# A chain of matrix products in sets: one round instead of two between the steps, and fewer sets under way

## The chip, the core and the metric

The kernel runs on one core of a Trainium2 chip, in one launch. The metric is the time of the launch in device microseconds; the median of three runs is compared. The core has five engines that run side by side, each in the order of its own instructions: TensorE (PE in the profile, with its weight loads as PEld), VectorE (DVE), ScalarE (ACT), GpSimd (POOL) and SyncE (SP), which only issues transfers here. An engine's instruction that needs another engine's result waits for it, and all that stands behind it on the same engine waits too.

## The reference

The input `x` has 32 images of 32 channels, each a 128 x 128 matrix, in float32. Two layers:

```python
def _L0_conv_ref(A):                      # NUM_ITER = 5
    normA = jnp.sqrt(jnp.sum(A2 * A2, axis=(1, 2)))
    Y = A2 / normA[:, None, None]
    Z = jnp.broadcast_to(I, A2.shape)
    for _ in range(NUM_ITER):
        T = 0.5 * (3.0 * I - jnp.matmul(Z, Y))
        Y = jnp.matmul(Y, T)
        Z = jnp.matmul(T, Z)
    return Y * jnp.sqrt(normA)[:, None, None]
...
x = x + _L0_conv_ref(_gn(x))
x = x + _L1_conv_ref(_gn(x), L1_conv_weights1, L1_conv_weights2)
```

`_gn` normalises each group of two channels by its mean and variance. The first layer is a Newton iteration towards the square root of each of the 1024 matrices. The second takes the real part of a two-dimensional Fourier transform, multiplies 32 x 32 low modes at two corners by weights that mix the channels, and transforms back.

## The kernel before

**Sets.** Four channels of an image are one set: 256 sets, eight to an image. `newton` (line 398) does the first layer for one set. It is a Python generator: each `yield` ends a step, and the loop that makes the program resumes many generators in turn, so that the yields decide in which order the instructions of different sets stand in the queues of the engines. Nothing of this runs on the chip: it is the order that is fixed here.

**Lanes and rounds.** The main loop (line 1000) counts rounds. In a round it visits the `LANES` = 9 lanes in turn. A free lane takes the next set if it is due: `due` grows by `FAR` = 27/9 or `NEAR` = 25/5 rounds with each start, and among near sets fewer than `LESS` = 5 may be under way. An occupied lane's generator is resumed once. A step that ends with `yield from rest` pauses for two rounds, since `rest = (None, None)`. At lane 1 of each round `step(preps)` is called, at lane 2 `step(specs)`, at lane 3 `step(posts)`, at lane 0 `step(prods)` in two rounds of three and `step(backs)` in the third.

**Far and near.** Sets of images 1 to 18 are far: 144 of them, the first stage. Image 0 (8 sets) and images 19 to 31 (104 sets, the second stage) are near. They differ in one transposition of the iteration, `quartic` (line 362), which is run twice in a set: a far set does it by a transposition of blocks on VectorE and a trip through DRAM, out and back on SP's queue; a near set on TensorE.

**The steps of a set**, with the names that the trace gives to the product (all products are line 305 but one; each is 8 matmul instructions in the trace, L415 with 256 columns, transpositions 4):

- mb by m (`ps<-x,b`), evicted to v by VectorE (L280); the second time `ps<-my,mb`
- far: v turned by VectorE (L371, `turn<-v`), stored to DRAM (L373), a pause, loaded back into w (L384, or four issues of L381), a pause, then on GpSimd w + r (L386). Near: v transposed on TensorE (L311, `ps<-ident,v`), evicted with r added to w by VectorE (L280)
- v by w (`ps<-w,v`), evicted to q by VectorE (L280)
- q by m (`ps<-x,q`), evicted to y by ScalarE (L404)
- q by y (`ps<-my,q`), evicted to m by ScalarE (L407)
- m transposed (L311, `ps<-ident,my`), evicted to mb by ScalarE (L272); GpSimd adds the scaled identity to it, r (L292 or L299)
- the second quartic, then q by y and m at once (L415, `ps<-my,q`), evicted by ScalarE in two instructions (L418) and four (L421)
- w by q (`ps<-q,t`), evicted to t by VectorE (L280)
- t by y (`ps<-y,t`), added to the input xt by VectorE (L425).

There is a pause after each of them, in the far quartic one more after each leg of the trip. A far set has 27 yields, a near one 25.

**Around the sets.** `fetch` loads a set's inputs on ScalarE's queue, `staged` scales them on ScalarE and GpSimd ahead of its start. `prep` (line 185) makes the statistics of two images at once: 16 steps with a load of xs on ScalarE's queue, three steps ahead, and two `bn_stats` (L206), then small steps with two square roots (`root`, line 151). `stage` (line 940) starts a `prep` when a set 12 before its images is staged, and finishes it at once, step by step, if it isn't done when its image is staged. `settle` stores a finished set to DRAM (L433), folds it on GpSimd (L438) and takes its statistics on VectorE (L443); `forward`, `summed` and `spectrum` (posts and specs) transform it. When a group of images is done (`GROUPS` = 20, 7, 3, 2), its spectra are multiplied by the weights (prods: `wide_products`, `small_products`, `last_products`) and transformed back (backs: `inverse`), between the near sets that still run. `weights` (line 751) loads the last group's weights on SP's queue into buffers as the last sets give them up: its `kinds` name a buffer and the round of the last set from which it is free.

Buffers come from pools with counts by name (`rooms`, line 256); until set 158 an extra pool is added to them.

Of the kernel before, what the change touches and what calls it, by code (L numbers as in the profile page):

```python
# [37 lines left out]
B = 32  # L38
C = 32
G = 16  # L40
LANES, LESS = 9, 5
FAR, NEAR = 27 / 9, 25 / 5
GROUPS = (20, 7, 3, 2)


# [6 lines left out]
FIRST = GROUPS[0] - 1  # L52
# [16 lines left out]
def conv_preact_kernel(  # L69
# [56 lines left out]
    early = first.enter_context(tc.tile_pool(name="early", bufs=1, side="right"))  # L126
# [16 lines left out]
    tail = False  # L143
# [7 lines left out]
    def root(v, n, tag):  # L151

        s0 = small.tile([P, n], F32, tag="root_0", name=f"{tag}_s0")
        nc.scalar.activation(s0, v, AF.Sqrt)
        q = small.tile([P, n], F32, tag="root_1", name=f"{tag}_q")
        nc.vector.reciprocal(q, s0)
        nc.vector.tensor_mul(q, q, v)
        nc.vector.tensor_tensor(q, q, s0, ALU.add)
        s = small.tile([P, n], F32, tag=f"{tag}_s", name=f"{tag}_s", bufs=2)
        nc.vector.tensor_scalar_mul(s, q, 0.5)  # L160
        return s
# [23 lines left out]
    def prep(bs, made):  # L185

        n = len(bs)
        nc_, ng = n * C, n * G
# [27 lines left out]
        v = small.tile([P, nc_ + ng], F32, tag="a_v", name=f"a_v{first_b}")  # L216
# [4 lines left out]
            vg, v[:, 0:nc_].rearrange("p (g c) -> p g c", c=2), AX.X, ALU.add  # L221
        )
        nc.vector.tensor_scalar(v[:, nc_:], vg, 0.5, EPS, ALU.mult, ALU.add)
        s = root(v, nc_ + ng, "a_r")
        iv = small.tile([P, nc_ + ng], F32, tag="a_inv", name=f"a_inv{first_b}")
        nc.vector.reciprocal(iv, s)
        yield
# [3 lines left out]
        nn = small.tile([P, ng, 2], F32, tag="a_d", name=f"a_n{first_b}")  # L231
# [5 lines left out]
        )  # L237
        nn = nn.rearrange("p g c -> p (g c)")
        nc.vector.tensor_scalar_mul(nn, nn, P * (1.5 / (EYE * QF)) ** 2)
        sn = root(nn, nc_, "a_t")  # L240

        off = small.tile([P, ng, 2], F32, tag="a_off", name=f"a_off{first_b}", bufs=2)
        nc.vector.tensor_tensor(
# [118 lines left out]
    def quartic(m, mb, r, far, more, wide):  # L362


        v = plus(m, -QA * MS, products(mb, m), "v", more)
        if far:


            t = four("turn", more)
            form = "p c (b i) -> p b c i" if wide else "p c (i b) -> p b c i"  # L370
            nc.vector.transpose(blocks(t), v.rearrange(form, b=4))  # L371
            held = dram.tile([P, 512], F32, name="turn", tag="turn", bufs=8)
            kept(nc.sync.dma_start(out=held, in_=t.rearrange("p c x -> p (c x)")))  # L373
            yield from rest
            w = four("w", more)
            wb = blocks(w).rearrange("p a c j -> p a (c j)")
            if wide:
                for b in range(4):
                    rows = slice(32 * b, 32 * b + 32)
                    src = held[:, P * b : P * b + P].rearrange("(a i) x -> i a x", a=4)  # L380
                    kept(nc.sync.dma_start(out=wb[rows], in_=src))  # L381
            else:
                src = held.rearrange("(a i) (b x) -> (i b) a x", a=4, b=4)
                kept(nc.sync.dma_start(out=wb, in_=src))  # L384
            yield from rest
            nc.gpsimd.tensor_tensor(w, w, r, ALU.add)  # L386
            w = blocks(w).rearrange("p a c j -> p c a j")
        else:
            yield from rest
            w = plus(transposed(v), 1.0, r, "w", more)  # L390
        yield from rest
        q = plus(products(v, w), QF / (16 * MS**4), eye, "q", more)
        yield from rest
        return q

    rest = (None, None)

    def newton(g, sn, xt, m, mb, r, far, more):

# [84 lines left out]
    def summed(b, st):  # L484
# [15 lines left out]
        v = small.tile([P, 2], F32, tag="b_v", name=f"b_v{b}")  # L500
# [2 lines left out]
        yield  # L503
        s = small.tile([P, 3], F32, tag="b_r", name=f"b_r{b}")
        nc.scalar.activation(s[:, 0:1], v[:, 0:1], AF.Sqrt)
        nc.vector.reciprocal(s[:, 1:2], s[:, 0:1])
        nc.vector.tensor_scalar(
            s[:, 2:3], v[:, 0:1], s[:, 1:2], s[:, 1:2], ALU.mult, ALU.mult
# [2 lines left out]
        r = small.tile([P, 1], F32, tag="b_inv", name=f"b_inv{b}")  # L511
# [4 lines left out]
    def spectrum(b, u):  # L516
# [16 lines left out]
        for i in range(2):  # L533
# [7 lines left out]
        v, r = scales.pop(b)  # L541
# [6 lines left out]
            AF.Identity,  # L548
            scale=r,
        )  # L550
        nc.vector.scalar_tensor_tensor(
            spec[0:C, 0, 0, 0:1], v[0:C, 1:2], r[0:C], spec[0:C, 0, 0, 0:1], ALU.mult, ALU.add
        )
        yield
        i, j = where[b]
# [195 lines left out]
    def weights():  # L751


        kinds = [("b", 2)] * 3 + [("x", 2), ("b", 4), ("x", 4), ("x", 10)]
        kinds += [("my", 11)] * 2 + [("r", 12)] * 4 + [("mb", 15)] * 2 + [("v", 15)] * 2
        kinds += [("w", 16)] * 2 + [("my", 16), ("r", 17)] + [("q", 19)] * 3
        first = B * C // 4 - 10
        spare = []
        for half in range(4, 2 * KK):
# [64 lines left out]
    holding = []  # L824
# [94 lines left out]
    posts = []  # L919
    specs = []  # L920
# [10 lines left out]
    rounds = 0  # L931
# [61 lines left out]
            yield  # L993

    preps.append(prep([0], made))
    coming = [((0, 0), [1])] + [((b - 2, 4), [b, b + 1]) for b in range(2, B, 2)]
    fetch(*fetches.pop(0))
    stage()
    fetch(*fetches.pop(0))
    while todo or any(lanes) or posts or specs or prods or backs:  # L1000
        tail = not todo and not any(lanes)
        if early and len(settled) >= MORE:
            change()
        for i in range(LANES):
# [16 lines left out]
            if lanes[i] is not None:  # L1021
# [3 lines left out]
                if next(steps, lanes) is lanes:  # L1025
                    lanes[i] = None
                    end(b, g, xt)
            if i == 1:
                step(preps)
            if i == 2 or tail:  # L1030
                step(specs)
            if i == 3 or tail:
                step(posts)
            if i == 0 and rounds % 3 or tail:
                step(prods)
            if i == 0 and (rounds % 3 == 0 or holding) or tail and not (posts or specs):
                step(backs)
        rounds += 1

# [68 lines left out]
```

## Time and profile before

| | us |
|---|---|
| median of 3 runs | 3051.56 (3039.8 to 3056.13) |
| the profiled run | 3040.36 |
| its span, first to last instruction | 3038.6 |
| mean granted TensorE clock | 0.984 |
| chain that ended last: PE / DMA / DVE | 75% / 10% / 9% of the span |
| DMA | 636.40 MB, mean 209 GB/s |
| POOL before r, waiting for mb (L299 behind ACT L272) | 278.8 in 66 waits |
| SP's queue before L373, waiting for the turned v, 152 to 1545 us | 466.1 in 185 waits |

The chain that ended last is followed back from the last instruction, at each step to what released it. A wait of an engine that isn't the bottleneck costs nothing by itself: SP and GpSimd may stand long before a transfer or an addition as long as the result is there when TensorE wants it. Matmul instructions are pipelined, so PE's busy time counts overlapping instructions once; the starts of two matmuls of the same kind that follow each other lie closer together than one of them lasts. In the timeline one product of eight matmuls is one line, "x8", with its start and the time to its end.

### The profile page before, as it was taken

To read this page: it belongs to the slowest core of one execution; us is meant where nothing else is said; L and a number is where in the kernel's file an instruction comes from. 1 tells how busy PE (TensorE), PEld (TensorE's weight loads), DVE (VectorE), ACT (ScalarE), POOL (GpSimd) and SP (SyncE) were. 2 spreads that over 40 slices of the span, in tenths; PEclk is the share of its full clock that TensorE was granted. 3 is DMA by queue.
4 is the path that set the end of the run, shared out by engine and by line. 5 is a ranking of instruction groups with operands and counts; after the bars stand their busy time and mean duration, and the time that the engine had idled before them with its cause. 6 is when DMAs were issued, how large, how long until landed. Compare 5 with 4: busy or idle time off the path is not lost.

```text
span 3038.6 us, 73447 instructions
## 1 busy us (share of the span) xinstructions
PE 2893.8 (95%) x27076; PEld 2684.5 (88%) x27076; DVE 2219.3 (73%) x4255; ACT 1636.0 (54%) x4187; POOL 1997.6 (66%) x2312
## 2 busy tenths in 40 slices
PE   6999999999999999999999999899999998999994
PEld 6899999999999999999999889798898887899983
DVE  6778787978787878778776745876877765876664
ACT  3565656565655656566544445455454454555552
POOL 4567677667777676777766435667677774677453
PEclk9999999999999999999999999999999999999996
DMA  5476766667675767576742566667667767775676
GB/s 179 148 224 199 220 213 205 212 207 224 197 237 188 251 184 246 185 229 198 228 136 81 183 204 214 232 206 239 229 225 242 245 231 242 227 222 189 198 240 217
DMA packets 476659, 636.40 MB, mean 209 GB/s; under 512 B 97040, under 2 KB 257296, under 8 KB 476304
## 3 DMA queue, kind: packets, MB, share of 16 engines
q1 hardware_dynamic: 363408, 425.88, 43.3%
q10 hardware_dynamic: 112896, 205.83, 21.4%
q8 instruction: 217, 3.56, 0.5%
q14 instruction: 138, 1.13, 0.1%
HBM read 402.42 MB, written 229.11 MB: 208 GB/s over the span
## 4 chain that ended last, share of the span: by engine, by line
PE 75%; DMA 10%; DVE 9%; POOL 2%; issue 2%; ACT 2%; SPq 1%; ACTq 0%; DVEq 0%; POOLq 0%
PE ps L305 49%; PE ps L415 12%; PE ps L311 6%; DMA w<-turn 3%; DMA xs<-in_xs 3%; PE ps L461 2%; PE ps L883 2%; DMA or<-od 1%; PE ps L612 1%; DVE yt L900 1%; PE ps L865 1%; DVE a_st L206 1%; DVE v L280 1%; DVE turn L371 1%; PE ps L682 1%
## 5 line engine op out<-in xcount | busy, mean ns | idle before, releaser
L386 POOL TENSOR_TENSOR w<-w,r 128x512 f32<-128x512 f32 x288 | 366.2, 1275 | 316.2 <-DMA w<-turn 262.1
L305 PE MATMUL ps<-w,v 128*128 128x128 f32 x4096 | 554.4, 279 | 19.0 <-POOL w L386 12.1
L339 ACT ACTIVATE b<-b,a_off,a_sc 128x128 f32<-128x128 f32 x1024 | 467.3, 491 | 177.5 <-issue 45.6
L305 PEld LDWEIGHTS ps<-w,v 128*128 128x128 f32 x4096 | 504.6, 193 | 35.1 <-POOL w L386 16.2
L415 PE MATMUL ps<-my,q 128*128 128x256 f32 x2048 | 493.3, 384 | 7.8 <-DVE q L280 5.2
L280 DVE SCALAR_TENSOR_TENSOR q<-ps,eye 128x512 f32<-128x512 f32 x512 | 348.8, 681 | 187.4 <-PE ps L305 181.1
L438 POOL TENSOR_TENSOR fold<-xt 128x256 f32<-128x256 f32 x512 | 364.3, 732 | 162.8 <-DVE xt L425 133.2
L833 POOL TENSOR_TENSOR yt<-yt,d 128x512 f32<-128x512 f32 x248 | 309.9, 1277 | 174.3 <-ACT d L895 137.7
L415 PEld LDWEIGHTS ps<-my,q 128*128 128x128 f32 x2048 | 373.2, 192 | 53.3 <-DVE q L280 4.7
L346 POOL TENSOR_SCALAR x<-xt,a_nm,a_sc 128x128 f32<-128x128 f32 x736 | 322.3, 450 | 18.3 <-DVE a_n L232 18.3
L299 POOL TENSOR_TENSOR r<-mb,eye 128x512 f32<-128x512 f32 x112 | 142.6, 1274 | 288.6 <-ACT mb L272 278.8
L418 ACT ACTIVATE t<-ps 128x256 f32<-128x256 f32 x512 | 192.6, 384 | 237.3 <-PE ps L415 229.4
L421 ACT ACTIVATE y<-ps,a_t_s 128x128 f32<-128x128 f32 x1024 | 312.4, 372 | 0.0
L305 PE MATMUL ps<-my,q 128*128 128x128 f32 x2048 | 276.7, 278 | 6.0 <-ACT d L895 3.9
L305 PE MATMUL ps<-x,b 128*128 128x128 f32 x2048 | 275.6, 278 | 6.7 <-POOL x L346 5.7
L305 PE MATMUL ps<-my,mb 128*128 128x128 f32 x2048 | 275.9, 278 | 6.5 <-ACT d L895 5.2
L305 PE MATMUL ps<-x,q 128*128 128x128 f32 x2048 | 276.0, 278 | 1.8 <-DVE q L280 1.6
L206 DVE BATCH_NORM_STATS2 a_st<-xs 128x6 f32<-128x256 f32 x512 | 195.4, 412 | 112.6 <-DMA xs<-in_xs 112.0
L305 PE MATMUL ps<-q,t 128*128 128x128 f32 x2048 | 274.5, 277 | 3.2 <-ACT d L895 1.6
L305 PEld LDWEIGHTS ps<-my,q 128*128 128x128 f32 x2048 | 260.8, 193 | 17.4 <-ACT d L895 4.5
L404 ACT ACTIVATE my<-ps 128x512 f32<-128x512 f32 x256 | 152.7, 596 | 229.2 <-PE ps L305 211.1
L305 PE MATMUL ps<-y,t 128*128 128x128 f32 x2048 | 273.9, 277 | 1.9 <-DVE t L280 1.6
(138 smaller groups left out, 5540.3 us busy)
## 6 DMA issues: line engine op xcount, KB each, us to landing
turn<-turn SPq DMA_DIRECT2D x288, 256.0 KB
b<-in_x ACTq DMA_DIRECT2D x256, 256.0 KB
xt<-in_xt ACTq DMA_DIRECT2D x256, 256.0 KB
xs<-in_xs ACTq DMA_DIRECT2D x256, 256.0 KB
mid<-xt SPq DMA_DIRECT2D x256, 256.0 KB
yt<-mid SPq DMA_DIRECT2D x128, 512.0 KB
out<-yt SPq DMA_DIRECT2D x120, 512.0 KB
w<-turn SPq DMA_DIRECT2D x144, 256.0 KB
```

What stands on the lines that cost most here:

```text
L206: nc.vector.bn_stats(st[:, 2 * k + j, :], tiles[k][:, j, :])
L280: nc.vector.scalar_tensor_tensor(s, ps, f, t, ALU.mult, ALU.add)
L305: nc.tensor.matmul(ps[:, j, :], lhsT[:, j], rhs[:, j], start=True, stop=True)
L311: nc.tensor.transpose(ps[:, j, :], t[:, j, :], ident)
L339: nc.scalar.activation(t, x, AF.Identity, bias=offset[:, c], scale=scale[:, c])
L346: nc.gpsimd.tensor_scalar(m[:, j, :], xt[:, j, :], nm[:, c // 2 : c // 2 + 1], sc[:, c : c + 1], ALU.add, ALU.mult,)
L386: nc.gpsimd.tensor_tensor(w, w, r, ALU.add)
L415: nc.tensor.matmul(both[j // 2][:, j % 2], q[:, j], my[:, j], start=True, stop=True)
L418: nc.scalar.mul(w[:, 2 * h : 2 * h + 2, :], both[h][:, :, 1, :], 1 / (MS * QF))
L421: nc.scalar.mul(y[:, j, :], both[j // 2][:, j % 2, 0, :], sn[:, c : c + 1])
L438: nc.gpsimd.tensor_tensor(f[:, :, 64 * half : 64 * half + 64], xt[:, :, 0:64], xt[:, :, 64:128], op)
L833: engine.tensor_tensor(yh, yh, d, op)
```

## The change

All of it is in the order of the instructions; none is added or removed on any engine, and no buffer count changes.

- The pause between steps is one round. The two pauses of the far quartic's trip through DRAM stay at two rounds, under a new name, `trip`.
- Six lanes instead of nine. A far set starts every 3 rounds, as before; a near set every 4 rounds instead of 5, while fewer than four are under way.
- `prep` is stepped in every second round once the first stage's extra pool is gone, and then starts two sets earlier. It has four more steps: before and after each square root on ScalarE. `summed` and `spectrum` have one more step each, after an instruction of ScalarE that VectorE continues.
- The products of the spectra are stepped in four rounds of five, the way back in two of five.
- The rounds from which `weights` may use a buffer follow the shorter life of a set.

```diff
-LANES, LESS = 9, 5
-FAR, NEAR = 27 / 9, 25 / 5
+LANES, LESS = 6, 4
+FAR, NEAR = 3, 4
...
         nc.scalar.activation(s0, v, AF.Sqrt)
+        yield
         q = small.tile([P, n], F32, tag="root_1", name=f"{tag}_q")
...
         nc.vector.tensor_scalar(v[:, nc_:], vg, 0.5, EPS, ALU.mult, ALU.add)
-        s = root(v, nc_ + ng, "a_r")
+        yield
+        s = yield from root(v, nc_ + ng, "a_r")
...
-        sn = root(nn, nc_, "a_t")
+        yield
+        sn = yield from root(nn, nc_, "a_t")
...
             kept(nc.sync.dma_start(out=held, in_=t.rearrange("p c x -> p (c x)")))
-            yield from rest
+            yield from trip
             w = four("w", more)
...
                 kept(nc.sync.dma_start(out=wb, in_=src))
-            yield from rest
+            yield from trip
             nc.gpsimd.tensor_tensor(w, w, r, ALU.add)
...
-    rest = (None, None)
+    rest = (None,)
+    trip = (None, None)
...
         nc.scalar.activation(s[:, 0:1], v[:, 0:1], AF.Sqrt)
+        yield
         nc.vector.reciprocal(s[:, 1:2], s[:, 0:1])
...
             scale=r,
         )
+        yield
         nc.vector.scalar_tensor_tensor(
...
-        kinds = [("b", 2)] * 3 + [("x", 2), ("b", 4), ("x", 4), ("x", 10)]
-        kinds += [("my", 11)] * 2 + [("r", 12)] * 4 + [("mb", 15)] * 2 + [("v", 15)] * 2
-        kinds += [("w", 16)] * 2 + [("my", 16), ("r", 17)] + [("q", 19)] * 3
+        kinds = [("b", 2)] * 3 + [("x", 2), ("b", 3), ("x", 3), ("x", 6)]
+        kinds += [("my", 6)] * 2 + [("r", 7)] * 4 + [("mb", 9)] * 2 + [("v", 9)] * 2
+        kinds += [("w", 9)] * 2 + [("my", 9), ("r", 10)] + [("q", 11)] * 3
...
-    coming = [((0, 0), [1])] + [((b - 2, 4), [b, b + 1]) for b in range(2, B, 2)]
+    coming = [((0, 0), [1])] + [((b - 2, 4 if b < FIRST else 2), [b, b + 1]) for b in range(2, B, 2)]
...
-            if i == 1:
+            if i == 1 and (early or rounds % 2):
                 step(preps)
...
-            if i == 0 and rounds % 3 or tail:
+            if i == 0 and rounds % 5 or tail:
                 step(prods)
-            if i == 0 and (rounds % 3 == 0 or holding) or tail and not (posts or specs):
+            if i == 0 and (rounds % 5 in (0, 2) or holding) or tail and not (posts or specs):
                 step(backs)
```

## The prediction

> **What bounds the kernel now.** I read the busy row first, then the span cut into its stages, then the waits stage by stage, and last the timeline, for what stands between two steps of one set.
>
> ```profile
> PE 2893.8 (95%) x27076; PEld 2684.5 (88%) x27076; DVE 2219.3 (73%) x4255; ACT 1636.0 (54%) x4187; POOL 1997.6 (66%) x2312
> ```
>
> TensorE (PE) is the busiest, but 95% hides two stages:
>
> ```profile
> core 0: us, PE busy (x) PEld busy (x) DVE busy (x) ACT busy (x) POOL busy (x), PEclk, DMA share, GB/s
> 152.00:1545.00 1393.00, 1379.39 (x11507) 1304.72 (x11506) 1109.09 (x2113) 831.38 (x2159) 1004.74 (x1109) 1.00 0.69 214
> 1545.00:1700.00 155.00, 155.00 (x1318) 146.93 (x1317) 105.64 (x223) 75.12 (x194) 86.45 (x117) 1.00 0.32 105
> 1700.00:2900.00 1200.00, 1143.28 (x12345) 1037.81 (x12344) 820.43 (x1543) 607.56 (x1532) 768.51 (x922) 0.99 0.68 222
> 2900.00:3039.00 139.00, 95.95 (x995) 81.95 (x993) 77.56 (x141) 53.55 (x133) 62.54 (x62) 0.81 0.65 226
> 0.00:152.00 152.00, 120.14 (x920) 113.06 (x921) 106.59 (x239) 68.42 (x170) 75.36 (x104) 0.97 0.50 163
> ```
>
> PE idles 14 us in the whole first stage (152 to 1545), 57 in the second (1700 to 2900), 32 at the start, 43 at the end. Nearly all that a faster kernel could gain lies in the second stage, the start and the end; in the first there is nothing to win and a cover to lose.
>
> What the cover is, in the timeline:
>
> ```profile
> 704.69 1.06 PE L305 MATMUL ps<-q,t 128*128 128x128 f32 x8
> ...
> 706.05 0.67 DVE L280 SCALAR_TENSOR_TENSOR t<-ps,eye 128x512 f32<-128x512 f32 x1
> ...
> 710.43 1.05 PE L305 MATMUL ps<-y,t 128*128 128x128 f32 x8
> ```
>
> The product of w and q ends at 705.8, VectorE (DVE) evicts it until 706.7, and the set's next product starts at 710.4: 3.7 us in which the eviction could have come later at no cost. Pairing every eviction with the product that reads it, over the 144 far sets, this slack is 3.4 to 5.4 us in the median at the steps without a trip through DRAM, and 1.5 to 3.3 us at the tenth percentile; at the two products behind a trip it is 3.3 and 3.7 us, and 0.2 and 0.8. Over the 104 later near sets it is 2.7 to 3.7 us, and 0.6 to 2.3. Who sits waiting meanwhile, in the first stage and in the second:
>
> ```profile
> POOL w L386 <- DMA w<-turn: 250.7, 116, 6.2
> ```
>
> ```profile
> DVE a_st L206 <- DMA xs<-in_xs: 39.9, 20, 6.3
> DVE spec L551 <- ACT spec L545: 12.5, 6, 4.5
> ```
>
> **The rounds, counted.** A far set had 27 pauses and one visit in which it ends: 28 rounds, nine lanes, 3.11 rounds a set. Starts lie 10.06 us apart, so a round is 3.23 us. Afterwards 18 pauses and the end make 19 rounds on six lanes, 3.17 a set, 3.18 us a round at the same pace. A step's distance falls from 6.46 to 3.18 us: 3.3 us less. A near set had 25 pauses and the end, five lanes, 5.2 rounds a set; starts lie 13.57 us apart, a round is 2.61 us. Afterwards a set starts every 4 rounds of 3.39 us; the distance falls from 5.22 to 3.39: 1.8 us less. The matrix work itself is unchanged, and so are its evictions, its DMAs and their kinds.
>
> **Far sets (144).** From each measured slack I take 3.3 us and keep what falls below zero. Short are 10 to 20% of most steps, 33% at q (L280, before L415) and 45% at m (ACT L407, before the transposition); of the two trips through DRAM, 50 and 43%. One wait of PE lets all that comes later catch up, so within one round I count the largest shortfall alone: 181 us over the stage without the trips, 357 with them. That is the upper end. The lower is -14, PE's whole idle time there. A count by hand says where in between. If the six lanes are taken in turn, the products follow each other as: mb by m of a new set, w by q, q by y, then t by y of the set whose w by q was just done. One product issues in 0.90 us (in the timeline the next starts at 1022.62 after 1021.72), so 1.80 us after the first ends PE wants t. VectorE has to evict v (0.68), turn it (0.91, L371) and evict t (0.68), which with some 0.14 us of handover is 2.4: 0.6 us late in every set, 86 us in 144. Half of 181 is 91. I take +90. What is late next is xt and, behind it on VectorE, the statistics; both are off PE's path.
>
> The trips keep two rounds for each leg, but from v to the product on w there are 5 rounds and not 6. POOL's L386 starts 11.8 us after v is evicted (median) and takes 1.28: 13.1, against 16.6 until the product before and about 13.3 after. Queued behind a waiting L386 on POOL are the staging (L346), the identity sums and the folds; SP's issues keep their order. I let these shortfalls hide behind the 0.6 us waits, and keep them as a rival.
>
> A page of the Trainium skill speaks for the change here ("DMA: Bandwidth & Descriptors", the section on what one DMA costs, "Fixed: setup + completion handling"): about 2.0 us plus the bytes over 436 GB/s, an estimate of 2.6 us for a 256 KB load. The trace has 5.3 us in the median from L384's issue to the POOL instruction that waited for it. By the page's figure the trip would be ready 2.7 us sooner and few trips would be short; the sum, which leaves the trips out, would be the same, and rival 1 would go.
>
> **Near sets (104).** The same count with 1.8 us gives 5 to 33% short and 110 us as the upper end. At the other end are waits that the change removes: with statistics every second round a load of xs has six rounds (20 us) and not three (8 us) to land, which ends the 39.9 us; the pause after the spectrum's scaling ends the 12.5 us. If PE felt all of it, -52. The tenth percentile of the slack is already down to 0.6 us at some steps, and ScalarE's six evictions behind L415 (2 of 0.38, 4 of 0.37 us) stand in front of another set's mb: I take two thirds of 110 as cost (75) and half of 52 as gain (26): +50.
>
> **The rest.** The added pauses issue nothing. A pair of images now takes 28 steps of statistics, not 24; in the near stage 14 sets of 4 rounds give 28 visits: just enough. If the count is one or two short, `stage` runs the last small instructions in a row, some 1 to 2 us for each of six pairs; I take 0, and 10 for the upper end. Products of the spectra are stepped 3.2 times a set, not 3.3, the way back 1.6, not 1.67: 20 images take 50 sets, not 48, of the 96 that follow; hidden by the sets, and two sets' time (27 us) at the end if they were not. At the start the first set runs alone for 4 steps and not 2.5, at about 2 us a step (0.90, an eviction of 0.68, handovers), then three lanes cover as five did: 0, within 5 either way. At the end the late weights (28 tiles of 256 KB) enter SP's queue over 12 rounds of the last set and not 25, ahead of loads of yt that VectorE waits for; in the chain that ended last, one of these weights stands with 5.5 us and the load of yt behind it with 8.7. Either may double or go: 0, between -14 and +14.
>
> The granted clock: 0.99 in the second stage with 5% of PE idle, 1.00 in the first with 1%. Where idle time doubles I add a hundredth of the 1200 us: +10. The skill's "TensorE: Matmul & The Clock Gate" (Part 1) has the clock halved only after an idle window of about 3.4 us, and waits of 0.6 us would then cost nothing in clock; by that the sum would be 10 less.
>
> **Sum.** The profiled run took 3040.36 us (span 3038.6); the median of the three shown is 3051.56, 0.4% above. 3040 + 90 + 50 + 10 = 3190.
>
> **Rivals.**
> 1. *The trips set the first stage's pace.* For it: L386 already waits for the DMA in 116 of its 278 instances there, 2.2 us each, and half the trips come out short. Against: a later PE makes the rounds longer, and with them the trip's five rounds. The largest shortfall of trips in each stretch of five rounds adds up to 131 us more: 3321.
> 2. *Faster: VectorE is freed in the second stage.* Place: L206 and L551 between 1700 and 2900. Price: -52, if evictions keep within one round elsewhere: 2988. For it: the median slack at every step is larger than what is taken off, and fewer sets may mean shorter queues on VectorE and ScalarE. Against: one step in five is not the median. It decides if PE's idle time in the first stage stays under about 50 us.
> 3. *Nothing to measure.* Lateness is queueing that adapts: evictions wait for PE today (VectorE idles 110 us before q in the second stage), and come as early as they are asked for. Then gains and losses of 20 or 30 us cancel: 3040.
>
> **How the numbers follow.** The forecast has 0.56, rival 1 0.14, rival 2 0.20, rival 3 0.10. The forecast's own range: 3090 to 3290 (90 + 50 between a third and twice). The whole range, 3000 to 3320, leaves out about half of rivals 1 and 2. Less than 0.5%, some 15 us, this measurement can't tell from no change. Slower are the forecast and rival 1, 0.70; faster is rival 2, 0.20; the same rival 3, 0.10.
>
> **What would show it.** Right: in 152 to 1545 PE's idle time grows from 14 to about 100 us, with t (L280) and m or mb as what PE waits for, and sets start about 10.7 us apart; VectorE's wait for xs in the second stage is gone. Wrong: PE still idle under 30 us in the first stage (rivals 2, 3), or idle time mainly behind POOL's L386 (rival 1), or waits in the last 140 us that move the total by more than 20.

## The result, and the profile after

The changed kernel takes 3396.59 us (median of 4 runs, 3392.31 to 3402.65) against 3052.57 (median of 4, 3039.8 to 3056.13) for the kernel before: 1.1154 times, interval 1.1128 to 1.118, some 345 us slower. The profiled run has a span of 3396.4 us; before it was 3038.6. The forecast was 3190, with a range that ended at 3320. The direction and the step that comes late were right, the size was not: the loss is more than twice the forecast.

Lines of the code have moved: L305 is now L308, L311 is L314, L280 is L283, L371 is L374, L386 is L389, L404 is L408, L407 is L411, L415 is L419, L418 is L422, L421 is L425, L425 is L429, L206 is L207. First the busy row of the page of after, and of the chain that ended last the row by engine:

```profile
PE 3012.0 (89%) x27076; PEld 2749.6 (81%) x27076; DVE 2244.8 (66%) x4259; ACT 1641.9 (48%) x4187; POOL 2000.0 (59%) x2308
...
PE 50%; DVE 18%; DMA 15%; issue 5%; ACT 5%; POOL 4%; ACTq 1%; SPq 1%; DVEq 0%; POOLq 0%
```

PE is still the busiest engine, but only half of the chain is now its own (75% before); VectorE has doubled its part, from 9 to 18%. VectorE's busy time hardly grew (2219.3 to 2244.8): it does the same work but for four additions, and PE stands waiting for it more often. (The counts of the two pages differ by these four: 2312 to 2308 instructions on GpSimd, 4255 to 4259 on VectorE. The code puts an addition of the way back on VectorE, and the store behind it on ScalarE's queue, once no set is under way, and more of them now come that late. So the change isn't in the order alone, but this part of it is small.)

The windows of after, by stage (columns as in the windows of before, with the same header):

```profile
0.00:193.00 193.00, 151.93 (x1147) 139.57 (x1148) 127.39 (x277) 82.61 (x211) 92.69 (x123) 0.99 0.47 149
193.00:1765.00 1572.00, 1415.99 (x11325) 1318.60 (x11324) 1113.09 (x2097) 829.31 (x2122) 991.88 (x1094) 0.98 0.60 187
1765.00:1870.00 105.00, 103.04 (x857) 96.69 (x856) 68.70 (x127) 48.56 (x125) 54.32 (x73) 1.00 0.29 89
1870.00:3293.00 1423.00, 1283.83 (x13117) 1147.50 (x13117) 880.66 (x1671) 652.77 (x1654) 827.16 (x993) 0.96 0.61 195
3293.00:3396.40 103.40, 57.20 (x639) 47.25 (x637) 54.96 (x91) 28.66 (x75) 33.98 (x28) 0.74 0.75 261
```

In the first stage PE idles 156 us (1572.00 - 1415.99) where it idled 14, and its granted clock went from 1.00 to 0.98. To compare like with like I cut every trace at the starts of sets (the first matmul of mb by m): up to the 17th set; 136 starts of the first stage; 103 of the second; and from the last set's start to the end.

| part | before, us | after, us | difference |
|---|---|---|---|
| to the 17th set | 162.0 | 193.1 | +31 |
| first stage, 136 sets | 1366.6 (10.05 a set) | 1571.7 (11.56) | +205 |
| second stage, 103 sets | 1402.5 (13.62) | 1528.7 (14.84) | +126 |
| from the last start to the end | 107.5 | 102.8 | -5 |

What PE waited for in the first stage, from the view of waits of after between 193 and 1765 us (engine and line, what it waited for, us in total, times, longest):

```profile
PE ps L308 <- DVE t L283: 126.3, 118, 3.7
...
POOL w L389 <- DMA w<-turn: 61.3, 63, 2.6
...
PE ps L419 <- DVE q L283: 12.2, 19, 1.9
...
PE ps L314 <- ACT my L411: 9.1, 4, 2.9
```

One wait is most of PE's idle time: the product t by y waits for t, in 118 of some 136 sets. GpSimd waits less for the trips through DRAM than before (250.7 us then, 61.3 now), and PE's own list has no wait for GpSimd that counts. How the wait comes about, from the timeline of after (start, us, instruction):

```profile
802.91 0.75 DVE L207 BATCH_NORM_STATS2 a_st<-xs 128x6 f32<-128x256 f32 x2 [0.71 <-DMA xs<-in_xs]
...
803.39 1.06 PE L308 MATMUL ps<-x,b 128*128 128x128 f32 x8
803.58 0.67 DVE L283 SCALAR_TENSOR_TENSOR v<-my,ps 128x512 f32<-128x512 f32 x1
...
804.28 0.71 DVE L374 STREAM_TRANSPOSE turn<-v 128x512 f32<-128x512 f32 x1
804.28 1.06 PE L308 MATMUL ps<-q,t 128*128 128x128 f32 x8
...
804.92 0.65 DVE L283 SCALAR_TENSOR_TENSOR v<-x,ps 128x512 f32<-128x512 f32 x1
...
805.18 1.06 PE L308 MATMUL ps<-my,q 128*128 128x128 f32 x8
805.60 1.10 DVE L374 STREAM_TRANSPOSE turn<-v 128x512 f32<-128x512 f32 x1
...
806.62 0.66 DVE L283 SCALAR_TENSOR_TENSOR t<-ps,eye 128x512 f32<-128x512 f32 x1
...
807.33 1.16 PE L308 MATMUL ps<-y,t 128*128 128x128 f32 x8 [1.10 <-DVE t L283]
```

PE's order is the one that the prediction counted on: x,b, then q,t, then my,q, then y,t. Ahead of t in VectorE's queue stand two v's and two turns, and it takes its queue in order: t begins at 806.62, 1.28 us after its product was done, and PE stands 1.10 us. The prediction saw one v and one turn ahead of t, and took VectorE to be free when x,b was done, at 804.45. Here it was not: VectorE was still turning the other set's v until 804.99, and began late on that one because statistics, themselves waiting for xs, stood in front.

This holds for a third of the sets only. A set without statistics near it, from the same timeline:

```profile
701.71 1.06 PE L308 MATMUL ps<-x,b 128*128 128x128 f32 x8
701.81 0.71 DVE L374 STREAM_TRANSPOSE turn<-v 128x512 f32<-128x512 f32 x1
...
702.61 1.06 PE L308 MATMUL ps<-q,t 128*128 128x128 f32 x8
...
702.88 0.69 DVE L283 SCALAR_TENSOR_TENSOR v<-x,ps 128x512 f32<-128x512 f32 x1 [0.35 <-PE ps L308]
703.50 1.06 PE L308 MATMUL ps<-my,q 128*128 128x128 f32 x8
...
703.60 1.11 DVE L374 STREAM_TRANSPOSE turn<-v 128x512 f32<-128x512 f32 x1
...
704.64 0.64 DVE L283 SCALAR_TENSOR_TENSOR t<-ps,eye 128x512 f32<-128x512 f32 x1
...
705.34 1.16 PE L308 MATMUL ps<-y,t 128*128 128x128 f32 x8 [0.78 <-DVE t L283]
```

Here the earlier turn is over before x,b is done (702.77), VectorE idles 0.35 us and takes v at once, as the prediction had it, and t by y is late all the same.

In the second stage the waits are spread (the view of waits of after between 1870 and 3293 us):

```profile
DVE a_st L207 <- DMA xs<-in_xs: 118.5, 48, 6.7
...
PE ps L308 <- DVE w L283: 29.1, 25, 3.9
...
PE ps L308 <- ACT t L422: 23.4, 12, 4.0
...
PE ps L308 <- ACT mb L275: 16.4, 28, 3.3
```

VectorE's wait for xs, which was to go, has grown from 39.9 us in the window shown of before to 118.5.

### The profile page after: what moved, and what is told of

Same layout as the page of the kernel before. It is cut to its first block, busy times and chain, and to the rows that moved or that the text cites. A ratio compares the mean times of both kernels' runs of the same rounds, so it can differ in the third digit from the quotient of the medians.

```text
span 3396.4 us, 72565 instructions
## 1 busy us (share of the span) xinstructions
PE 3012.0 (89%) x27076; PEld 2749.6 (81%) x27076; DVE 2244.8 (66%) x4259; ACT 1641.9 (48%) x4187; POOL 2000.0 (59%) x2308
## 3 DMA queue, kind: packets, MB, share of 16 engines
q14 instruction: 135, 1.11, 0.1%
## 4 chain that ended last, share of the span: by engine, by line
PE 50%; DVE 18%; DMA 15%; issue 5%; ACT 5%; POOL 4%; ACTq 1%; SPq 1%; DVEq 0%; POOLq 0%
PE ps L308 33%; PE ps L419 8%; DMA xs<-in_xs 8%; DVE turn L374 4%; PE ps L314 4%; DVE v L283 3%; DVE t L283 2%; DVE yt L906 2%; DMA turn<-turn 1%; PE ps L465 1%; ACT b L342 1%; DMA yt<-mid 1%; DVE a_st L207 1%; PE ps L889 1%; DVE q L283 1%
## 5 line engine op out<-in xcount | busy, mean ns | idle before, releaser
L308 PE MATMUL ps<-w,v 128*128 128x128 f32 x4096 | 572.2, 285 | 47.2 <-DVE w L283 38.8
L308 PEld LDWEIGHTS ps<-w,v 128*128 128x128 f32 x4096 | 520.6, 199 | 59.5 <-DVE w L283 39.4
L342 ACT ACTIVATE b<-b,a_off,a_sc 128x128 f32<-128x128 f32 x1024 | 456.2, 485 | 135.3 <-issue 77.4
L419 PE MATMUL ps<-my,q 128*128 128x256 f32 x2048 | 493.3, 384 | 19.7 <-DVE q L283 19.2
L419 PEld LDWEIGHTS ps<-my,q 128*128 128x128 f32 x2048 | 371.6, 191 | 73.6 <-DVE q L283 26.0
L283 DVE SCALAR_TENSOR_TENSOR q<-ps,eye 128x512 f32<-128x512 f32 x512 | 348.9, 681 | 109.7 <-PE ps L308 99.1
L308 PE MATMUL ps<-y,t 128*128 128x128 f32 x2048 | 300.3, 291 | 135.0 <-DVE t L283 130.7
L389 POOL TENSOR_TENSOR w<-w,r 128x512 f32<-128x512 f32 x288 | 363.0, 1274 | 72.7 <-DMA w<-turn 69.1
L308 PEld LDWEIGHTS ps<-y,t 128*128 128x128 f32 x2048 | 257.7, 197 | 167.2 <-DVE t L283 159.2
L408 ACT ACTIVATE my<-ps 128x512 f32<-128x512 f32 x256 | 153.2, 599 | 422.4 <-PE ps L308 417.7
L283 DVE SCALAR_TENSOR_TENSOR v<-my,ps 128x512 f32<-128x512 f32 x256 | 174.6, 682 | 249.1 <-ACT y L425 154.7
L207 DVE BATCH_NORM_STATS2 a_st<-xs 128x6 f32<-128x256 f32 x512 | 195.2, 416 | 209.9 <-DMA xs<-in_xs 209.5
L295 POOL TENSOR_TENSOR r<-b,eye 128x512 f32<-128x512 f32 x144 | 183.5, 1274 | 238.8 <-ACT b L342 238.8
L275 ACT COPY mb<-ps 128x512 f32<-128x512 f32 x256 | 151.8, 593 | 343.9 <-PE ps L314 313.5
L425 ACT ACTIVATE y<-ps,a_t_s 128x128 f32<-128x128 f32 x1024 | 313.9, 371 | 0.0
L422 ACT ACTIVATE t<-ps 128x256 f32<-128x256 f32 x512 | 193.4, 384 | 237.7 <-PE ps L419 225.5
L308 PEld LDWEIGHTS ps<-my,mb 128*128 128x128 f32 x2048 | 265.8, 195 | 51.7 <-ACT mb L275 30.1
L308 PE MATMUL ps<-my,mb 128*128 128x128 f32 x2048 | 283.6, 282 | 24.9 <-ACT mb L275 20.3
L308 PE MATMUL ps<-q,t 128*128 128x128 f32 x2048 | 281.0, 280 | 25.0 <-ACT t L422 23.6
```

What stands on the lines that cost most here:

```text
L207: nc.vector.bn_stats(st[:, 2 * k + j, :], tiles[k][:, j, :])
L283: nc.vector.scalar_tensor_tensor(s, ps, f, t, ALU.mult, ALU.add)
L295: nc.gpsimd.tensor_tensor(blocks(r).rearrange("p a c j -> p c a j"), mb.rearrange("p c (a j) -> p c a j", a=4), eye.rearrange("p c (a j) - ...
L308: nc.tensor.matmul(ps[:, j, :], lhsT[:, j], rhs[:, j], start=True, stop=True)
L342: nc.scalar.activation(t, x, AF.Identity, bias=offset[:, c], scale=scale[:, c])
L419: nc.tensor.matmul(both[j // 2][:, j % 2], q[:, j], my[:, j], start=True, stop=True)
```

## The experiments

All twelve, with the parts of the table above. "Half clock" is the time for which the trace shows the clock granted at one half ("all" is the whole trace, some 2 us outside the span included). The ratio is to the kernel before, run beside it on the same chip: its median was 3042.53 us beside the first four edits, 3049.72 beside the next four, 3042.53 beside the last four.

| kernel | median, us | ratio [95%] | to 17th set | us a set, 1st / 2nd stage | last start to end | half clock, 1st / 2nd / all |
|---|---|---|---|---|---|---|
| before | 3052.57 | | 162.0 | 10.05 / 13.62 | 107.5 | 0 / 34 / 98 |
| after | 3396.59 | 1.1154 [1.1128, 1.118] | 193.1 | 11.56 / 14.84 | 102.8 | 55 / 102 / 217 |
| late_turn | 3283.24 | 1.0804 [1.0763, 1.0846] | 190.5 | 10.71 / 14.76 | 104.2 | 10 / 89 / 167 |
| t_pause | 3297.89 | 1.0841 [1.0817, 1.0865] | 194.6 | 10.92 / 14.71 | 100.3 | 38 / 99 / 196 |
| nine_lanes | 3107.13 | 1.0218 [1.0201, 1.0235] | 167.5 | 10.06 / 12.80 | 253.1 | 3 / 10 / 193 |
| small_edits | 3044.48 | 1.001 [0.9991, 1.0029] | 160.4 | 10.01 / 13.61 | 111.6 | 3 / 31 / 98 |
| nine_paced | 3073.29 | 1.0081 [1.0059, 1.0103] | 168.5 | 10.06 / 13.75 | 117.9 | 0 / 61 / 121 |
| seven_lanes | 3159.6 | 1.037 [1.033, 1.0409] | 176.4 | 10.40 / 14.30 | 101.3 | 7 / 99 / 164 |
| rounds_only | 3363.76 | 1.104 [1.1001, 1.1079] | 189.3 | 11.56 / 14.59 | 98.9 | 48 / 79 / 180 |
| y_split | 3395.28 | 1.114 [1.1102, 1.1177] | 191.6 | 11.56 / 14.71 | 104.5 | 55 / 96 / 215 |
| six_two | 3379.96 | 1.1094 [1.1053, 1.1136] | 196.3 | 11.63 / 14.69 | 87.3 | 99 / 82 / 244 |
| stats_every | 3372.31 | 1.1081 [1.1048, 1.1114] | 192.7 | 11.54 / 14.57 | 103.6 | 51 / 75 / 190 |
| no_pauses | 3383.44 | 1.1114 [1.1084, 1.1144] | 188.8 | 11.61 / 14.70 | 99.9 | 61 / 82 / 199 |
| near_six | 3056.42 | 1.0052 [1.0033, 1.007] | 156.6 | 10.05 / 13.47 | 136.0 | 0 / 44 / 119 |

**Is it VectorE's order? (late_turn)** The changed kernel with the turn of v one round later, and the leg behind it one round shorter, so that a set stays as long. The turns are kept in this order in the program, which puts t ahead of them.

```diff
         if far:
+            yield from rest
             t = four("turn", more)
...
-            nc.vector.transpose(blocks(t), v.rearrange(form, b=4))
+            kept(nc.vector.transpose(blocks(t), v.rearrange(form, b=4)))
             held = dram.tile([P, 512], F32, name="turn", tag="turn", bufs=8)
...
-            yield from trip
+            yield from rest
             w = four("w", more)
```

> The changed kernel with the block transpositions of the far sets (L371 of before) moved one round later and pinned there on VectorE, behind t; the trip's first leg is one round instead of two, so a set still has 18 pauses and TensorE's order is the same, instruction for instruction. Theory A (t is late because v, turn, v, turn stand in front of it on VectorE): TensorE's wait for t falls from 1.12 us a set to under 0.4, some 100 us less in the first stage, total about 3290; what is late next is w, behind a trip that starts 1 to 2 us later. Theory B (one round is too short for every step, whatever the order): other waits take the place of t's, total within 30 us of 3397.

The time fell by 113 us to 3283.24, all of it in the first stage: 11.56 to 10.71 us a set, 115 us over 136. The wait for t fell from a mean of 1.12 us a set to 0.30. (This is measured by the matmuls: how much later t by y starts than the usual spacing after the matmul before it. The view of waits counts only the time in which PE stands idle, 126.3 us in the first stage of after, and this way it is 152.) The timeline of late_turn, where VectorE takes t ahead of both turns:

```profile
824.13 1.06 PE L308 MATMUL ps<-q,t 128*128 128x128 f32 x8
...
825.12 0.67 DVE L283 SCALAR_TENSOR_TENSOR v<-x,ps 128x512 f32<-128x512 f32 x1
...
825.71 0.68 DVE L283 SCALAR_TENSOR_TENSOR t<-ps,eye 128x512 f32<-128x512 f32 x1
...
826.32 1.70 DVE L374 STREAM_TRANSPOSE turn<-v 128x512 f32<-128x512 f32 x2
...
826.45 1.16 PE L308 MATMUL ps<-y,t 128*128 128x128 f32 x8 [0.37 <-DVE t L283]
```

No work was taken away, two turns only stand behind t. PE's order is the same too: in both kernels one product, q by y of another set, stands between w by q and t by y in all 136 sets. So the order of VectorE's queue is the cause of over half of the first stage's loss, with the half clock that the waits brought along (55 to 10 us); the other 90 us (10.71 against 10.05) are left.

**A pause only where it waits (t_pause).** Two rounds, not one, between w by q and t by y of a far set.

```diff
         t = plus(products(w, q), -0.5 * EYE / (1.5 * QF), eye, "t", more)
-        yield from rest
+        yield from (trip if far else rest)
         nc.vector.tensor_tensor(xt, products(t, y), xt, ALU.add)
```

> The changed kernel with two rounds instead of one between t and the product that reads it, in far sets only: a set has 19 pauses, 20 rounds on six lanes. Theory A: the 165 us that TensorE waited for t in the first stage go, less some 30 for other products that move closer together; 3397 - 130 = 3265. Theory B: the waits go to q and m, total over 3340.

The time fell by 99 us, less than the 130 that were expected, with 86 in the first stage. The waits of PE in the first stage of t_pause (195 to 1790 us):

```profile
PE ps L314 <- ACT my L411: 22.2, 22, 5.0
PE ps L308 <- POOL w L389: 17.9, 22, 2.6
PE ps L308 <- DVE q L283: 16.9, 26, 3.0
...
PE ps L308 <- DVE t L283: 2.2, 2, 1.2
```

The wait for t is gone (126.3 to 2.2 us), and others have come: six lanes hold no more work than before, and a set that lingers at one step gives less cover at the others.

**Is it the pauses or the sets? (nine_lanes, nine_paced, seven_lanes, six_two)** nine_lanes is the changed kernel's way of pausing with nine sets, the count of before:

```diff
-FAR, NEAR = 27 / 9, 25 / 5
+FAR, NEAR = 19 / 9, 13 / 5
...
-    rest = (None, None)
+    rest = (None,)
+    trip = (None, None)
```

with the small edits, statistics in every round, and the products of the spectra and the way back stepped on other rounds, since a round with nine sets that each do more is longer.

> One round between steps as in the changed kernel, but nine far and five near sets under way as before (a far set starts every 19/9 rounds, a near one every 13/5), with statistics, products and the way back stepped so often that a set gets as much of them as before. Theory C (what counts is the work of other sets between two steps of one: 0.64 of a far set before, 0.32 in the changed kernel, 0.47 here): far sets start every 10.2 to 10.6 us, total 3080 to 3170. If the pause itself counted, in rounds, it would stay above 3300.

The windows of nine_lanes, the first stage with the 143 us behind it in which PE doesn't idle, and the second:

```profile
167.00:1678.00 1511.00, 1494.89 (x12472) 1414.85 (x12471) 1206.00 (x2276) 895.04 (x2301) 1073.52 (x1199) 1.00 0.66 204
1678.00:3000.00 1322.00, 1235.76 (x13302) 1123.64 (x13301) 889.96 (x1686) 653.43 (x1637) 771.55 (x941) 0.97 0.64 207
```

The first stage is whole again: PE idles 16 us of 1511, and a set takes 10.06 us. One round or two between the steps makes no difference there when nine sets are under way. The second stage, 12.80 us a set, looks better than before's 13.62 but isn't: the way back fell behind, and 253.1 us came after the last start, not 107.5. nine_paced steps the products of the spectra and the way back more often, to tell the one from the other:

```diff
-LANES, LESS = 6, 4
-FAR, NEAR = 3, 4
+LANES, LESS = 9, 5
+FAR, NEAR = 19 / 9, 13 / 5
...
-            if i == 0 and rounds % 5 or tail:
+            if i == 0 or i == 4 and rounds % 3 == 0 or tail:
                 step(prods)
-            if i == 0 and (rounds % 5 in (0, 2) or holding) or tail and not (posts or specs):
+            if i == 0 or i == 4 and rounds % 3 == 0 or tail and not (posts or specs):
```

> As nine_lanes, with the products of the spectra and the way back stepped four times in three rounds instead of once or less, so that a set gets 3.47 steps of each as before; in nine_lanes 145 us of the way back had slipped behind the last set. Theory C (the work of other sets between two steps is what counts): first stage as before (1367 us), second stage and end together 1490 to 1515 as before (1510), total 3020 to 3055. Rival (one round with many sets is better than two rounds, since TensorE waited only 28 us in the second stage of nine_lanes, against 63 before): under 3015.

With the way back in step the second stage is at 13.75 us a set and the time at 3073.29: 0.8% slower than before (ratio 1.0081, interval 1.0059 to 1.0103), outside the expected band and far from the rival's gain. With the same sets under way one round is nearly what two are, and no better. seven_lanes puts in one lane more than the changed kernel has, starts near sets every 13/4 rounds and not every 4, and steps the statistics, the products and the way back in every round:

```diff
-LANES, LESS = 6, 4
-FAR, NEAR = 3, 4
+LANES, LESS = 7, 4
+FAR, NEAR = 19 / 7, 13 / 4
```

> The changed kernel with seven far lanes (a set every 19/7 rounds) and four near sets (every 13/4): the distance between two far steps is 3.7 us at the pace of before, not 3.2. Theory A and C: the wait for t falls by about that half microsecond, far sets start every 10.7 to 10.9 us (11.56 in the changed kernel, 10.06 in nine_lanes), near every 14.0 to 14.4 (14.84), total 3200 to 3260. If the number of sets mattered by a threshold (a lane too few), it would be near one of the two ends, 3110 or 3390.

3159.6 us: this takes back 237 of the 344 us, more than was expected; stats_every below puts the statistics' part at some 24. The first stage takes 10.40 us a set, and the wait for t is 0.11 us, from 1.12. The loss is no straight line in the number of sets: 10.06, 10.40 and 11.56 us for nine, seven and six.

The traces show why. Between w by q and t by y of one set PE has these products of other sets in the first stage: five or six before, three to five in nine_lanes, two to four in seven_lanes, and in after one, in all 136 sets. From the start of w by q to that of t by y it is 6.15 us before and 2.75 after (medians), and of the 2.75 only 1.80 are two products' work. The average of 3.18 us a round doesn't hold at this place: six sets started three rounds apart fall into step. Counted in the code, a set takes 19 rounds on its lane, and starts come three rounds apart (once in six, four). So when one stands at w by q, another has just done the first product of a new set ahead of it, one is at q by y, and three are inside a trip and have no product for PE in between. With 19/7 rounds between starts the sets do not stay in one such pattern. Six sets at another spacing were not run with one round, so how much is the number of sets and how much their falling into step is not told apart.

That leaves the other corner, six sets that pause two rounds:

```diff
-FAR, NEAR = 3, 4
+FAR, NEAR = 28 / 6, 26 / 3.25
...
-    rest = (None,)
-    trip = (None, None)
+    rest = (None, None)
```

with the small edits taken back and the other steps paced to match.

> The kernel before (two rounds between all steps) with as few sets under way as the changed kernel has: six far sets, one started every 28/6 rounds, and 3.25 near sets, one every 8 rounds; statistics started four sets later, products and the way back stepped as often per set as before. Theory C (work of other sets between two steps: 0.43 of a far set, against 0.32 with one round and 0.64 before): the wait for t is short (some 0.3 us a set), but the trips get 6 of 28 rounds of a shorter life and w is late instead; far sets every 10.4 to 11.2 us, total 3150 to 3280. If two rounds in themselves were the cure, it would be within 40 of 3050; if six sets in themselves were the illness, within 40 of 3380.

3379.96 us, as slow as the changed kernel within 17 us. The waits of six_two between 196 and 1880 us, GpSimd's first:

```profile
POOL w L386 <- DMA w<-turn: 229.2, 93, 7.6
...
PE ps L305 <- POOL w L386: 101.7, 76, 3.4
```

The wait for t is nearly gone, and PE now waits for the trips instead: with two rounds everywhere, the legs of the trip have no more than the other steps. (Between w by q and t by y there are three to five products here.) The place is the one that was expected, the size is not. That the two kernels with six sets come out within 17 us of each other is no law of six sets, since they wait at different steps, and late_turn, with six too, is 113 us faster than after. Of the four corners, nine sets take 3043 to 3053 us with two rounds and 3073 with one, six sets 3380 with two and 3397 with one.

**The rest of the change (small_edits, rounds_only, stats_every, no_pauses).** small_edits puts the new pauses and the slower statistics on the kernel before; rounds_only takes both out of the changed kernel, stats_every the slower statistics alone, no_pauses the new pauses alone.

```diff
-            if i == 1 and (early or rounds % 2):
+            if i == 1:
                 step(preps)
```

(rounds_only and stats_every, where the statistics also start as early as in the kernel before)

```diff
         nc.scalar.activation(s0, v, AF.Sqrt)
-        yield
         q = small.tile([P, n], F32, tag="root_1", name=f"{tag}_q")
```

(rounds_only, no_pauses; likewise at the other four new pauses)

> The kernel before with the small edits alone: pauses around the square roots and behind the spectrum's scaling, statistics every second round in the near stage, started two sets earlier. Pauses, lanes and pacing of products as before. My prediction had 26 us of gain from them in the second stage: 3027. Rival: what they take from VectorE's waits was hidden, within 10 us of 3052. If they were part of the loss it would be slower by more than 20.

> The changed kernel without the small edits: no pauses around the square roots, statistics every round, started as before. Theory: they are worth nothing here either, 3385 to 3415. Rival: with short distances VectorE's waits for a square root now reach TensorE, 3420 to 3440; or the statistics every second round took part in the loss, under 3375.

> The changed kernel with statistics in every round and started as before, the added pauses around the square roots and behind the spectrum's scaling kept. rounds_only, without all small edits, was 33 us faster than the changed kernel, 26 of it in the second stage. If the halved pace costs this (bn_stats now spread over 56 of 64 rounds of a pair, in front of evictions that have no slack), 3360 to 3375; if the pauses do, 3390 to 3400.

> The changed kernel without the added pauses, statistics in every second round kept. The counterpart of stats_every: 3390 to 3400 if the halved pace costs the 33 us, 3360 to 3375 if the pauses do; both in the middle if each takes a part.

On the kernel before they are worth nothing that shows (ratio 1.001, interval 0.9991 to 1.0029). On the changed kernel they cost: rounds_only takes 3363.76 us, 33 less than after; stats_every 24 less, no_pauses 13 less (this last with an interval that overlaps that of after, so it may be nothing). The first of these is mostly the second stage (14.84 to 14.59 us a set, 26 us), and by stats_every most of it comes with the halved pace of the statistics. The forecast had them as a gain of 26 us.

**ScalarE's evictions ahead of mb (y_split).** Two of the four y's behind L419 of a near set go to VectorE.

```diff
-            nc.scalar.mul(y[:, j, :], both[j // 2][:, j % 2, 0, :], sn[:, c : c + 1])
+            if j % 2 and not far:
+                nc.vector.tensor_scalar_mul(y[:, j, :], both[j // 2][:, j % 2, 0, :], sn[:, c : c + 1])
+            else:
+                nc.scalar.mul(y[:, j, :], both[j // 2][:, j % 2, 0, :], sn[:, c : c + 1])
```

> The changed kernel with two of the four evictions of y behind L415 (L421 of before) moved from ScalarE to VectorE, in near sets only: 0.74 us a set less in front of mb and t on ScalarE. My prediction named these evictions as what mb waits for. If so, TensorE's waits for mb (26 us in the second stage) and t by ScalarE (29 us) halve and the second stage is 25 to 45 us shorter, total about 3360. Rival: ScalarE is late for other reasons (the copies of the way back) and VectorE is the tighter engine, no gain or a loss within 20.

3395.28 us: nothing gained. PE's time lost ahead of my,mb fell from 32 to 15 us in the second stage, as it would if ScalarE's queue was what held it; ahead of w,v, which waits for VectorE, it grew from 47 to 52, and ahead of q,t, whose factor ScalarE evicts at L422, from 29 to 36. The queue was the right one, but relief at one step came back as waits at others.

**More sets where PE idles (near_six).** The kernel before, with six near sets under way and not five.

```diff
-LANES, LESS = 9, 5
-FAR, NEAR = 27 / 9, 25 / 5
+LANES, LESS = 9, 6
+FAR, NEAR = 27 / 9, 26 / 6
```

> The kernel before with six near sets under way instead of five (one every 26/6 rounds). Theory C carried one step further: more work between two steps takes some of the 63 us that TensorE waits in the second stage and of the 34 us of half clock there, 15 to 40 us, total 3010 to 3035. Rival: those waits come from the way back and its loads, or buffers run out with six sets: within 10 of 3050, or slower.

The second stage gains 15 us (13.62 to 13.47 a set), and 28 come back after the last start (107.5 to 136.0), since the way back falls behind: 1.0052 times, interval 1.0033 to 1.007, where a gain was expected. No kernel of these beat the one before.

## Why the prediction was wrong in size

**What bounds it, and where PE waits: right.** PE, two stages with different limits, the first with nothing to win and a cover to lose. PE's order and the engine queue in which t comes late are as counted by hand; the first stage's wait is for t, and mb is among those of the second; the end changes by -5 us (0 was said, within 14). Of the pace, "about 10.7 us apart" was said, and 11.56 came.

**The far sets: the step that failed.** "0.6 us late in every set, 86 us in 144", taken as +90; measured were +205. The hand count had the right place and was too small in its parts, the time that VectorE needs before t and the time that PE has until it wants t. The mean wait for t is 1.12 us, and 136 times that is 152 us.

- Where none of the `bn_stats` on xs stands on VectorE from 2 us before w by q starts until t (91 of 136 sets), VectorE is free as the count had it, and PE waits 0.91 us. The turn behind v takes 1.11 us; 0.91, which was reckoned, is the mean of two forms, of 0.71 and 1.11 us. And PE wants t 1.64 us after x,b is done, not 1.80: three products start 0.90 us apart, but the first is done 1.06 us after its start (3 x 0.90 - 1.06). These two make 0.96 of the 0.6.
- In the other 45 sets, where statistics stand on VectorE, it is 1.5 us.

All products of the sets together lost 187 us by this measure, against 14 before. That is near the 181 that pairing slack with loss had given and that was halved, but this is luck: in the trace of before that pairing gives, step by step, 28 us at t, 85 at m and 57 ahead of L415; measured are 151 at t, 10 at m and 16 ahead of L419, as that line now is. It took 3.3 us from every step alike, while at t the distance between the products is 1.80. late_turn, which moves only the turns, got 115 back.

**The near sets.** +50 was said, 75 of cost less 26 of gain. The waits grew by 105 us (62 to 167), close to the 110 that the count gave as its upper end. That count went by a near set of 25 pauses; by the code it has 23, and in the trace of before it lives 4.39 starts from its first product to its last, which is 22 rounds with a start every 5. So a round was 2.71 us, not 2.61, and the distance fell by 2.0 us, not 1.8. The gain didn't come: the four runs on the small edits show them at nothing on the kernel before and at 33 us of cost after. Of the two waits, the spectrum's is gone as said (12.5 to 0.3 us), that for xs is not. Its step, "a load of xs has six rounds (20 us) and not three (8 us) to land", is wrong by its own measure: in the second stage xs is first read some 5 us after its load was issued, in the median of 80 loads, before the change and after it. In 18 of the 80 before, and in 62 after, the next load had not even been issued by then, where three were to be under way. Stepping the statistics more slowly moved the load and its use together. What keeps the issue so late wasn't tried.

**The clock.** +10 was said, and 0 by the page that was cited. The trace of after has 217.1 us at half clock, before 97.6. If half of the time at half clock is lost, it is (217.1 - 97.6) / 2, some 60 us, 27 of them in the first stage, where before had none, and 34 in the second. It is an estimate; no run separates the clock from the waits that bring it about. In late_turn both go together, 55 to 10 us in the first stage.

**The start.** 0 was said, within 5; it is +31. It was argued that three lanes cover as five did. nine_lanes (167.5), seven_lanes (176.4) and after (193.1) against 162.0 fit the same loss of cover as elsewhere; no run takes it apart.

**Rivals.** The trips did not set the pace in the changed kernel, where GpSimd waits 61.3 us for them in the first stage and PE hardly for GpSimd; in six_two, with the trip no longer than other steps, they did. The prediction's 2.6 us for a load, from the Trainium skill ("DMA: Bandwidth & Descriptors", under "Anatomy of one DMA — SWDGE (gpsimd) path"), is a fit that the page gives for transfers issued from GpSimd, while these are issued on SP's queue: the trace's 5.3 us is the number that holds here. VectorE freed in the second stage: fell, with the wait for xs. Nothing to measure: fell, with PE's idle time.

**Together.** 173 us more of waits and 27 of clock in the first stage make 200 of 205; 105 and 34 in the second make 139 of 126 (a wait at half clock is in both); 31 at the start, -5 at the end. The forecast had 140 for the waits of both stages, where 278 were measured, 10 for the clock, where the estimate is 60, and nothing for the start.

What stays open: how six sets would do that don't fall into step; how the second stage's loss divides by cause, since no run took away one of its waits without feeding another; and the start.

## What to carry to other kernels

Count the distance between two dependent steps in the work of other sets that lies between them, step by step, and not in pauses or in an average round. Nine sets with one round kept the first stage at 10.06 us a set. No single average orders the runs: between two plain steps seven_lanes has 7/19 = 0.37 of a set and takes 10.40 us, six_two has 12/28 = 0.43 and takes 11.63. What six_two is short of is the trip, where its PE waits: from v to the product on w it has 6 rounds, 1.29 sets, where seven_lanes has 5 rounds, 1.84 sets, and before 6 rounds, 1.93 sets. So look for the step with the least between, and see whether the starts of the sets make it the same step in every set. There, write out the queue of the engine that evicts, with everything that is in it and each instruction at the time of its own form; moving two instructions behind the late one gave 113 us back here. A total that comes out near the measured one proves a count only if its parts do too.

## What the hardware showed unexpectedly

Single waits of 2 to 3 us can be followed by a stretch at half clock. The products of after around a wait of 2.17 us (timeline, PE alone):

```profile
829.10 1.06 PE L308 MATMUL ps<-my,q 128*128 128x128 f32 x8
832.33 1.55 PE L308 MATMUL ps<-y,t 128*128 128x128 f32 x8 [2.17 <-DVE t L283]
833.67 1.92 PE L308 MATMUL ps<-w,v 128*128 128x128 f32 x8
835.38 1.06 PE L314 MATMUL ps<-ident,my 128*128 128x128 f32 x4
```

From 833.0 the granted clock is one half for 3.41 us: the first product takes 1.55 and the next 1.92 us instead of 1.06. The first stage of after has 54.6 us of this in 15 stretches, 14 of them 3.41 us long; before had none. Twelve of the 15 begin less than 2 us after a product that came 1.5 to 3.9 us late. But of the 20 matmuls of this stage that came 2 us late or more, only ten are followed by such a stretch; what decides between them these traces don't show. The Trainium skill, "TensorE: Matmul & The Clock Gate", states in Part 1 under "What's actually happening" that the clock halves after at least one idle window of about 3.4 us; by that alone a wait of 2.17 us would have cost nothing more. The same page, under "A second HAM failure mode: psum-queue depth-cycling", tells of a kernel whose frequent short idle times made the clock swing between half and full. The traces here agree with the second passage, and the prediction had drawn on the first alone.
